# A key or value job that begins in front of the last bank of transposes, in the last block's cross attention of a four-block transformer kernel

## The chip, the cores and the metric

The kernel runs on one core of one Trainium2 chip. A core has a matrix engine (TensorE, "PE" in the profile; its weight loads are "PEld"), three engines for elementwise work (VectorE or "DVE", ScalarE or "ACT", GpSimd or "POOL") and a queue that only issues transfers (SyncE or "SP"). The metric is the device time in microseconds (us) of one execution; less is better. All arithmetic is in 32-bit floats.

## The reference

Four transformer blocks run one after the other on `x` of shape 8 x 112 x 256, with a context of shape 8 x 375 x 192. The first two blocks are self attention, cross attention to the context and a gated feed-forward layer. The third is cross attention alone. The fourth, on which the change works, is

```python
h = _layernorm(x, ln1_w, ln1_b)            # self attention, causal, 16 heads of 16
...
x = x + sa @ proj_w + proj_b
h = _layernorm(x, ln2_w, ln2_b)            # cross attention, 16 heads of 16
q = (h @ q_w + q_b).reshape(B, T, H, HD).transpose(0, 2, 1, 3)
k = (enc @ k_w + k_b).reshape(B, S, H, HD).transpose(0, 2, 1, 3)
v = (enc @ v_w + v_b).reshape(B, S, H, HD).transpose(0, 2, 1, 3)
attn = jnp.einsum('bhtd,bhsd->bhts', q, k) * scale
...
x = x + ca @ out_w + out_b
h = _layernorm(x, ln3_w, ln3_b)
h = jax.nn.gelu(h @ mlp1_w + mlp1_b, approximate=False)
x = x + h @ mlp2_w + mlp2_b
```

with B = 8 batches, T = 112 rows of each, S = 375 context positions, H = 16 heads.

## The kernel before

**Steps.** Attention is cut into 176 steps (0 to 175). In the last block a self-attention step takes 8 heads of one batch, and a cross-attention step 4 heads (four steps to a batch). In Python, each step is a handful of items, made by `add_step` (L913):

- `S`: the score matmuls (L986) into two double-bank PSUM tiles, and, on VectorE, the mask and the row minimum (L934), and half of the step's exponentials on ScalarE (L942). For a cross step these are 4 minima, and 2 of its 4 exponentials, which this text calls the early ones.
- `E`: the other half of the exponentials, the late ones.
- `T`, by bank: four PE transposes of the exponentials (L1013) into one PSUM bank, and the copy of that bank to SBUF. A cross step has three banks (the 375 positions in chunks of 128, 128 and 119): banks 0 and 2 are copied by ScalarE (L1022) and bank 1 by VectorE (L1019). The first bank needs all four exponentials.
- `PV`: the products with the values (L1043), which read the copies.

**Other items.** Projections of the queries (L725), normalizations (`norm`: a product at L669, then statistics on VectorE and GpSimd), their transposes (`hT`, L637), the scaling by the softmax sums (`N`, L1089), and the feed-forward matmuls (`ff`, L1296; made by `last_ff`, L1285) are fillers: the planner puts them between the parts of the steps. ScalarE's exact-GELU passes over the feed-forward result (L1323) are the items `gelu`; the first covers 512 columns in two instructions, the second 256 columns.

**Jobs.** The keys and values of the context (192 deep) are made by jobs in two halves. `begin` issues two matmuls over the first 128 rows (L791 for keys, L866 for values) into two PSUM banks; the second half, called the finish here, issues the two matmuls over the other 64 rows (L800, L875) into the same banks, and then their evacuation. The last block's cross attention has 8 key jobs and 12 value jobs.

**What sets the order.** TensorE's order is the planner's, written out as the program is built (`manual_schedule` for PE, L315). The other engines' queues are ordered by the framework's scheduler, except where the kernel pins an instruction (`keep_in_program_order`, among others for the late exponentials and the GELU passes). [...] The planner's loop (L1468 to L1491) goes through the steps: in iteration i it closes the open jobs (their finish), issues `S` of step i + 2, in every second iteration the `PV` of two steps, then the banks `T` of step i + 1 with fillers between them, `E` of step i + 2, more fillers, and opens jobs at the very end (`open_jobs`, L179). It has a clock of its own with estimated costs: `left` is the filler time due in an iteration, by the fillers' due times, and `ready` (L258) names the filler that can go now, or none. So a shift of one item moves the clock and with it where later fillers go.

**PSUM.** All matmul results other than scores share four banks (`ps_m`, L314), handed out in the order in which they come free. A begun job holds two of them until it is evacuated.

Of the kernel before, what the change touches and what calls it, by code (L numbers as in the profile page):

```python
# [299 lines left out]
def kernel(ctx: ExitStack, tc: tile.TileContext, a: dict, out: bass.AP):  # L300
# [20 lines left out]
    plan = Plan(RINGS, ARENA, lambda k: 512 if k[0] == "v" else S if k[0] == "k" and k[1] in (1, 4, 6, 8) else 4 * T)  # L321
# [845 lines left out]
    def first_of(st, b):  # L1167
        return at[(st, b, 0)]
# [284 lines left out]
    for seg in range(3):  # L1453
        lo, hi = cuts[seg], cuts[seg + 1]


        for s in (lo, lo + 1):
            for k in plan.items[("S", s)].uses + plan.items[("PV", s)].uses:
                mk = plan.maker.get(k)
                if mk is None or plan.items[mk].done:  # L1460
                    continue
                if plan.items[mk].begin is not None:
                    plan.require(mk)
                else:
                    plan.drain(mk)
        if seg == 0:
            plan.require(("hT", 0, 1))
        for i in range(lo - 2, hi):  # L1468
            plan.step = i
            left = plan.pace(i, seg)  # L1470
            if i < lo:

                left = max(left, 6.5)
            plan.close_jobs()
            if lo <= i + 2 < hi:
                plan.main(("S", i + 2))

            if lo <= i < hi and (i - lo) % 2 == 1:
                plan.main(("PV", i - 1))
                plan.main(("PV", i))  # L1480
            if lo <= i + 1 < hi:
                n = steps[i + 1]
                share = left / (n + 2)
                left -= plan.fill(2 * share, 1.5 if i < lo else 0.0)
                for k in range(n):
                    plan.main(("T", i + 1, k))
                    left -= plan.fill(min(left, share))
            if ("E", i + 2) in plan.items and lo <= i + 2 < hi:
                plan.main(("E", i + 2))
            plan.fill(left, 1.5 if i < lo else 0.0)  # L1490
            plan.open_jobs(1 if i + 1 >= first_of(8, 0) else 2, i + 3.5, seg)  # L1491
    plan.step = len(steps)
    while plan.pending:
        plan.drain(plan.pending[0].key)
# [35 lines left out]
```

## Time and profile before

| what | us |
|---|---|
| median of 3 runs (1654.88 to 1657.93) | 1656.19 |
| the profiled execution | 1655.89 |
| its span, first to last instruction | 1654.1 |
| span from 1463 to 1606: last block's attention where jobs are begun, up to the last score matmuls | 143.0, of which PE busy 138.0 |
| span from 1606 to 1614.7: the last steps' transposes and products | 8.7, of which PE busy 6.9 |
| span from 1614.7 to 1651.5: feed-forward tail | 36.8, of which PE busy 36.2 |

The page gives the busy time of each engine; a group line gives the source line, the engine, the operation, the count, the mean, and the idle time before it with what ended it. PE is busy for 99% of the span, DVE 49%, ACT 47%, POOL 43%. Matmul ends are modelled in this profile, so a busy PE does not mean a PE at its fastest; the start times are what is recorded. A timeline row reads: start, length, engine, line, operation, tiles, count, and in brackets the idle time of that engine just before it and what ended it. Rows of several instructions are merged, the start is that of the first. The granted TensorE clock is 1.00 (full) in every slice of the span.

### The profile page before, as it was taken

How to read it: one execution, taken by the hardware profiler on the slowest of the kernel's cores; microseconds unless marked ns; L12 is line 12 of the kernel's file. 1: busy time of each engine (PE TensorE's matmuls, PEld its weight loads, DVE VectorE, ACT ScalarE, POOL GpSimd, SP SyncE). 2: the span in 40 equal slices, each digit the busy share in tenths (PEclk: the TensorE clock that was granted, in tenths of full speed). 3: DMA queues.
4: the chain of work that ended last, by engine and by line, in shares of the span. 5: the costliest groups of instructions: out<-in, count | busy, mean ns of one | idle time of the engine just before them, and what ended most of it. 6: DMA issues, size and time to landing. Idle time of an engine off the chain costs nothing.

```text
span 1654.1 us, 30129 instructions
## 1 busy us (share of the span) xinstructions
PE 1633.6 (99%) x11784; PEld 1142.1 (69%) x11784; DVE 813.6 (49%) x2166; ACT 781.9 (47%) x2448; POOL 718.5 (43%) x687
## 2 busy tenths in 40 slices
PE   9999999999999999999999999999999999999999
PEld 8777666666667878676666665676666666766667
DVE  3554454544522344545454552344455556677752
ACT  3453444444531444434444452144445555687772
POOL 1324555556632223355565580364564448422110
PEclk9999999999999999999999999999999999999999
DMA  6012020000101011000000010100000000000000
GB/s 186 5 54 54 3 87 1 1 26 1 52 29 46 1 30 52 27 1 30 1 2 26 1 46 29 33 23 1 1 2 1 16 1 27 30 2 2 2 2 23
DMA packets 26613, 39.50 MB, mean 24 GB/s; under 512 B 1527, under 2 KB 21623, under 8 KB 26471
## 3 DMA queue, kind: packets, MB, share of 16 engines
q1 hardware_dynamic: 26231, 37.40, 7.3%
q8 instruction: 93, 1.52, 0.4%
q14 instruction: 49, 0.40, 0.1%
q10 hardware_dynamic: 240, 0.17, 0.0%
HBM read 35.88 MB, written 0.92 MB: 22 GB/s over the span
## 4 chain that ended last, share of the span: by engine, by line
PE 90%; ACT 3%; DVE 3%; POOL 2%; issue 1%; ACTq 0%; POOLq 0%; DVEq 0%
PE mm L669 13%; PE mm L703 11%; PE mm L1043 10%; PE s L986 10%; PE mm L1013 9%; PE mm L791 8%; PE mm L825 7%; PE mm L1261 6%; PE mm L800 5%; PE mm L834 4%; PE mm L750 3%; ACT pr L942 2%; PE mm L1296 2%; POOL pr L963 1%; PE mm L637 1%
## 5 line engine op out<-in xcount | busy, mean ns | idle before, releaser
L963 POOL TENSOR_SCALAR pr<-pr,rinv 112x375 f32<-112x375 f32 x384 | 468.7, 1239 | 333.5 <-DVE rinv L960 333.4
L954 ACT ACTIVATE pr<-s,nm 112x375 f32<-112x375 f32 (+1 forms) x640 | 302.0, 489 | 169.4 <-DVE nm L948 167.1
L355 DVE COPY arena<-mm 128x375 f32<-128x375 f32 (+4 forms) x189 | 113.4, 609 | 286.3 <-PE mm L800 137.1
L1013 PEld LDWEIGHTS mm<-ident,pr 112*128 112x128 f32 (+2 forms) x1920 | 209.1, 151 | 50.2 <-issue 19.7
L1013 PE MATMUL mm<-ident,pr 112*128 112x112 f32 (+2 forms) x1920 | 235.4, 264 | 6.8 <-ACT pr L942 3.3
L347 ACT COPY arena<-mm 128x375 f32<-128x375 f32 (+4 forms) x179 | 92.8, 519 | 294.4 <-PE mm L800 139.0
L948 DVE TENSOR_REDUCE nm<-s 112x2 f32<-112x750 f32 (+1 forms) x224 | 206.3, 958 | 51.1 <-PE s L986 47.8
L986 PE MATMUL s<-arena 64*112 64x375 f32 (+3 forms) x1792 | 211.7, 394 | 0.1
L1043 PEld LDWEIGHTS mm<-wT,arena 128*64 128x64 f32 (+5 forms) x3840 | 159.9, 129 | 36.9 <-issue 20.1
L347 ACT COPY wT<-mm 119x448 f32<-119x448 f32 (+2 forms) x235 | 123.8, 535 | 124.5 <-PE mm L1013 124.4
L1043 PE MATMUL mm<-wT,arena 128*64 128x112 f32 (+5 forms) x3840 | 179.5, 261 | 0.0
L986 PEld LDWEIGHTS s<-arena 64*112 64x112 f32 (+1 forms) x1792 | 113.9, 172 | 79.5 <-issue 29.9
L942 ACT ACTIVATE pr<-pr,nm 112x112 f32<-112x112 f32 (+1 forms) x256 | 124.6, 491 | 33.5 <-DVE nm L934 33.5
L969 POOL TENSOR_TENSOR pr<-pr,rinv 112x896 f32<-112x896 f32 x32 | 53.9, 1685 | 197.3 <-DVE rinv L967 179.7
L954 ACT ACTIVATION_READ_ACCUMULATOR pr<-s,nm 112x1 f32 x640 | 133.2, 208 | 0.0
L599 POOL TENSOR_TENSOR rs<-ve,mhalf 128x1 f32<-128x1 f32 x70 | 39.7, 567 | 203.3 <-DVE ve L597 203.3
L960 DVE RECIPROCAL rinv<-sums 112x1 f32<-112x1 f32 x384 | 62.5, 163 | 90.1 <-ACT pr L954 89.6
L825 PE MATMUL mm<-L_xattn_Wv,ctxA 128*128 128x512 f32 (+1 forms) x192 | 92.4, 600 | 2.2 <-ACT wT L347 1.3
L791 PE MATMUL mm<-ctxA,L_xattn_Wk 128*128 128x375 f32 x256 | 91.4, 481 | 0.0
L673 DVE TENSOR_TENSOR x<-mm,x 128x256 f32<-128x256 f32 x70 | 29.6, 423 | 115.9 <-PE mm L669 115.9
L703 PE MATMUL mm<-hT,L_xattn_Wq 128*128 128x224 f32 x384 | 83.0, 360 | 0.0
L353 DVE TENSOR_SCALAR arena<-mm 128x448 f32<-128x448 f32 (+2 forms) x65 | 42.0, 646 | 82.0 <-PE mm L834 47.0
(134 smaller groups left out, 2326.5 us busy)
## 6 DMA issues: line engine op xcount, KB each, us to landing
L_xattn_Wo<-in_L_xattn_Wo_dram SPq DMA_DIRECT2D x3, 1024.0 KB, 15.2
L_xattn_w_ff<-in_L_xattn_w_ff_dram SPq DMA_DIRECT2D x3, 1024.0 KB, 5.2
L_xattn_Wv<-in_L_xattn_Wv_dram SPq DMA_DIRECT2D x4, 512.0 KB, 4.5
L_xattn_Wq<-in_L_xattn_Wq_dram SPq DMA_DIRECT2D x2, 1024.0 KB, 4.7
L_xattn_Wp<-in_L_xattn_Wp_dram SPq DMA_DIRECT2D x2, 1024.0 KB, 5.4
L_xattn_wq<-in_L_xattn_wq_dram SPq DMA_DIRECT2D x2, 1024.0 KB
L_xattn_wo<-in_L_xattn_wo_dram SPq DMA_DIRECT2D x2, 1024.0 KB, 5.3
L_xattn_mlp_w<-in_L_xattn_mlp_w_dram SPq DMA_DIRECT2D x2, 1024.0 KB, 5.3
```

The lines of the kernel that those rows point to most:

```text
L347: nc.scalar.copy(dst, src)
L669: nc.tensor.matmul(ps[:, :D], lhsT=oT[:, c, t * P : (t + 1) * P], rhs=got[wv or w][:, c, :], start=(c == 0), stop=(c == n - 1),)
L703: nc.tensor.matmul(ps[:, i * 2 * T : (i + 1) * 2 * T], lhsT=got[w][:, k, m * P : (m + 1) * P], rhs=hT[:, k, lo:hi], start=(k == 0), stop=( ...
L791: nc.tensor.matmul(ps[:, :S], lhsT=got[wv][:, (2 * u + i) * P : (2 * u + i + 1) * P], rhs=ctxA[:, cols], start=True, stop=False,)
L825: nc.tensor.matmul(ps[: KCH[c][1], :], lhsT=lhs(ctxA, slice(0, KA), c), rhs=got[w][:, hf * 512 : (hf + 1) * 512], start=True, stop=False,)
L942: return nc.scalar.activation(pr, pr, AF.Exp, bias=nm, scale=-1.0, accum_out=bsums[(st, b)][:, h : h + 1])
L948: nc.vector.tensor_reduce(nm[:, :, :ns], sv, AX.X, ALU.max, negate=True)
L954: nc.scalar.activation(pr[:, bk, sl, :], sv[:, bk, sl, :], AF.Exp, bias=nm[:, bk, sl : sl + 1], accum_out=sums[:, bk, sl : sl + 1],)
L963: nc.gpsimd.tensor_scalar_mul(pr[:, bk, sl, :], pr[:, bk, sl, :], rinv[:, bk, sl : sl + 1])
L986: nc.tensor.matmul(tiles[i][:, n % 2, (n // 2) * nk : (n // 2 + 1) * nk], lhsT=qap(h), rhs=kap(h), start=True, stop=True,)
L1013: nc.tensor.transpose(pt[:kl, m * T : (m + 1) * T], cell[h][:, c * P : c * P + kl], ident[:T, :T])
L1043: nc.tensor.matmul(po[p0 : p0 + dp, blk * T : (blk + 1) * T], lhsT=got[vk][:kl, hv * dp : (hv + 1) * dp], rhs=wt, start=(c == 0 and par(h) ...
```

## The change

In the last block (from the iteration whose transposes are those of the first step of its cross attention), in front of a step's last bank of transposes, the planner asks whether any filler is ready. If none is, it opens one job there, sets the remaining filler time of the iteration to nothing, and issues no filler in what is left of the iteration. Where a job was opened in this way, the opening at the end of the iteration opens no second one.

```diff
@@ -1483,12 +1483,19 @@
                 share = left / (n + 2)
                 left -= plan.fill(2 * share, 1.5 if i < lo else 0.0)
                 for k in range(n):
+                    if k == n - 1 and i + 1 >= first_of(8, 0) and plan.ready() is None:
+
+
+                        plan.open_jobs(1, i + 3.5, seg)
+                        left = 0.0
                     plan.main(("T", i + 1, k))
-                    left -= plan.fill(min(left, share))
+                    if not plan.opened:
+                        left -= plan.fill(min(left, share))
             if ("E", i + 2) in plan.items and lo <= i + 2 < hi:
                 plan.main(("E", i + 2))
-            plan.fill(left, 1.5 if i < lo else 0.0)
-            plan.open_jobs(1 if i + 1 >= first_of(8, 0) else 2, i + 3.5, seg)
+            if not plan.opened:
+                plan.fill(left, 1.5 if i < lo else 0.0)
+            plan.open_jobs(1 if plan.opened or i + 1 >= first_of(8, 0) else 2, i + 3.5, seg)
```

As built, nothing differs ahead of step 137. From there on, 13 of the 20 jobs begin in front of the last bank (in the iterations 144, 146, 147, 150, 152, 156, 157, 158, 160, 162, 164, 165 and 166). Fillers shift by an iteration or more: among others the queries `q` of batches 4/5 and 6/7, the norms, and the feed-forward items `ff`, which go to iterations 168 to 171 where they were in 166 to 170. In the last iteration of transposes (174), which has no job to open, the fillers before step 175's last bank are now `hT` (the transposes of rows 512 to 767) and the first `gelu`; before the change both came after it, the `hT` behind the products.

## The prediction

> **What bounds the kernel now.** I read first the busy time of each engine in stretches of the last block (columns: stretch, its length, then PE, PEld, DVE, ACT and POOL busy with instruction counts, granted clock, DMA share, GB/s):
>
> ```profile
> 1463.00:1606.00 143.00, 138.02 (x1467) 90.64 (x1469) 102.40 (x390) 106.78 (x334) 27.65 (x47) 1.00 0.01 2
> 1606.00:1614.71 8.71, 6.89 (x132) 5.17 (x124) 5.36 (x19) 6.43 (x16) 2.92 (x4) 1.00 0.01 2
> 1614.71:1651.50 36.79, 36.24 (x184) 31.86 (x184) 9.37 (x23) 8.19 (x12) 2.51 (x3) 1.00 0.07 22
> ```
>
> PE sets the time in all three. Where jobs move (first row) it is idle for 143.0 - 138.0 = 5.0 us: no order of the same instructions can win more there. The tail (last row) has 0.55 us of PE idle in 36.8, so whatever delays its start delays the end by as much.
>
> Next, who ends PE's waits from 1460 to 1606 (us in total, times, longest):
>
> ```profile
> PE mm L1013 <- ACT pr L942: 2.3, 8, 0.4
> PE mm L791 <- ACT wT L1022: 1.1, 2, 0.6
> PE mm L669 <- ACT wT L1022: 1.0, 2, 0.5
> PE mm L866 <- ACT wT L1022: 0.7, 3, 0.3
> PE mm L791 <- DVE x L673: 0.2, 1, 0.2
> ```
>
> 2.3 of the 5.3 is transposes (L1013) waiting for exponentials, which a moved job does not feed. The rest, 3.0, is jobs and norms that want a PSUM bank and wait for ScalarE's copy of a transposed bank (L1022). These are what the change can reach.
>
> Then single rows: weight loads with the idle time ahead of them.
>
> ```profile
> 1508.86 0.30 PEld L791 LDWEIGHTS mm<-ctxA,ctx_w 128*128 128x128 f32 x2 [1.24 <-ACT wT L1022]
> 1529.45 0.30 PEld L791 LDWEIGHTS mm<-ctxA,ctx_w 128*128 128x128 f32 x2 [1.06 <-ACT wT L1022]
> 1539.77 0.94 PEld L1013 LDWEIGHTS mm<-ident,pr 112*128 112x128 f32 x9 [0.45 <-ACT pr L942]
> ```
>
> In the first two, the second matmul of a key job waits for the PSUM bank that bank 0 of the transposes left; its copy stands on ScalarE behind two early exponentials of the next step (0.60 each). Loads run ahead of matmuls, so PE itself is late by less: measured from start to start, by 0.81 and 0.63.
>
> Last, the end of the attention (step 175), the place that decides my forecast:
>
> ```profile
> 1611.08 1.11 PE L1013 MATMUL mm<-ident,pr 112*128 112x112 f32 x9 [0.28 <-ACT pr L942]
> ...
> 1611.43 0.53 ACT L1022 COPY wT<-mm 128x448 f32<-128x448 f32 x1 [0.41 <-PE mm L1013]
> ...
> 1612.13 1.36 PE L1043 MATMUL mm<-wT,arena 128*32 128x112 f32 x48
> 1612.29 0.53 ACT L1022 COPY wT<-mm 119x448 f32<-119x448 f32 x1 [0.32 <-PE mm L1013]
> 1612.84 1.28 ACT L1323 ACT_TABLE_LOAD   x1
> 1613.42 0.42 PEld L637 LDWEIGHTS mm<-ident,xn 128*128 128x128 f32 x4 [0.17 <-issue]
> ...
> 1614.13 3.71 ACT L1323 ACTIVATE oT<-oT 128x2048 f32<-128x2048 f32 x2
> ...
> 1614.71 7.20 PE L1296 MATMUL mm<-hT,L_xattn_mlp_w 128*128 128x256 f32 x32 [0.64 <-DVE hT L642]
> ```
>
> ScalarE copies banks 0 and 2 of step 175, then loads the GELU table and makes two long GELU passes, under the products and the feed-forward matmuls.
>
> **The change, part by part.** It adds and removes no instruction of PE, DVE, ACT or POOL in sum; no DMA moves, and the queues of SP and POOL keep their order. The built order shows three kinds of shift.
>
> *1. Thirteen jobs begin before the last bank.* The start-to-start spacing in the timeline gives 0.38 for a bank of transposes, 1.26 for a key job's begin, 0.86 for a value job's. Before, PE does banks 1 and 2 and the job's first matmul (0.38 + 0.38 + 0.63 = 1.39) before it wants bank 0's place; after, in most cases, bank 1 and the whole begin (0.38 + 1.26 = 1.64) before the last bank of transposes wants it. So a waiting key job gains 0.25, a value job 0.05 (1.24 against 1.19). Site by site: iterations 144 and 158 gain 0.25 and 0.3, 156 0.1; 146 loses 0.1; the rest waited for nothing. The price: bank 2's copy on ScalarE comes 0.86 to 1.26 later, and the late exponentials of the next step are queued behind it; the next bank 0 waits for these. In ten of the thirteen iterations a pair of `PV` (1.29) stands between, and the late exponentials ended 1.3 to 3.7 ahead of their transposes: hidden. Iteration 147 is a self step whose last bank VectorE copies; 165 is hidden; 157 loses 0.1. Were the cover gone, each would cost up to 0.9. **Sum: gain 0.5.**
> Three key evacuations also go from ScalarE (0.55) to VectorE (0.57), which is idle for 40 of the 143 us: nothing.
>
> *2. Fillers shift.* (a) The queries of batches 6/7 stood between the transposes of step 160 and `S` of 162; their two evacuations on ScalarE held up the late exponentials of 161, and PE lost 0.41 + 0.50 at the transposes (third row above) and 0.15 at the job. Now they follow `S` 162: **gain 1.1**. (b) Steps 151 and 153 lose the filler ahead of their transposes (a norm, 0.97; queries of 4/5, 1.62). From the end of step 150's or 152's bank 2 to the last late exponential it takes 0.2 + 0.53 + 2 x 0.60, and PE has only one `S` (0.83) to put there: new waits of 0.85 and 1.05. At the bank 0 copies behind them 0.3 and 0.5 replace 0.41 and 0.44. The queries, now ahead of step 155's bank 0, remove 0.17 + 0.81 there. 1.83 - 2.70: **loss 0.9**. (c) The norm ahead of job 164 goes behind the products, so that job waits 0.85 and the transposes 0.53 where they waited 0.48; 0.45 is new at 166/167, which lose their feed-forward fillers; these fill 171/172 instead and remove 0.50 and 0.65 around step 173. 1.63 - 1.83: **loss 0.2**.
>
> Parts 1 and 2 gain 0.5 + 1.1 - 0.9 - 0.2 = 0.5 us. Bounds: 5.0 gained (all idle of the first row), and 4 lost (new waits of the size of (b) in every fourth step).
>
> *3. The last iteration.* The norm of tile 5 is now 1.2 us earlier on the planner's clock, so `hT` and the first `gelu` (which asks for 4 us after the last `S`) become ready one bank early and go in front of step 175's bank 2. In the built ScalarE queue, the copy of that bank now stands behind the table load and the two passes. Step 175's last four products (8 of the 48 PE instructions of L1043) need it, and all feed-forward matmuls are queued behind them. From the rows: bank 0's copy ends at 1611.43 + 0.53 = 1611.96; table 1.28: 1613.24; passes 3.71: 1616.95; bank 2's copy 0.53: 1617.48; four products, 0.18, and the change to the next matmul, 0.24: L1296 starts at 1617.9 instead of 1614.71. **Loss 3.2.** The 0.64 wait on hT that goes away is in this difference. PE would have run out of work near 1613.6 (bank 0 ends 1611.2, then 0.38 + 0.5 + 0.4 for banks and `hT`, 1.1 for 40 products), so it stands still for 3.9 us.
>
> Two rules of the Trainium skill bear on this stall, both against the change. The row has the table load at 1.28, starting 0.02 after the copy's end; "ScalarE: Activation LUTs" (What ACT_TABLE_LOAD costs) adds a drain, 2.66 for a switch. By the rule the stall is 1.4 longer and the loss 4.6. I take the row: it is this switch. Second, the clock. No PE pause before the end is over 1.3 us, but behind the last matmul (1650.9) there is one:
>
> ```profile
> 1651.00:1654.10 3.10, 0.00 (x0) 0.00 (x0) 0.42 (x1) 0.00 (x0) 0.00 (x0) 1.00 0.13 42
> 1654.00:1656.00 2.00, 0.00 (x0) 0.00 (x0) 0.00 (x0) 0.00 (x0) 0.00 (x0) 0.70 0.00 0
> ```
>
> 0.70 is 0.8 us at full and 1.2 at half clock: it fell at 1654.8, 3.8 us after the last matmul. "TensorE: Matmul & The Clock Gate" (Part 1) says the same of a free-running idle window of about 3.4 us, and that about 3.4 us of work at half clock restore it. With the row's 3.8, a 3.9 us stall just reaches it; if it does, an estimate from the page is 3.4 / 2 = 1.7 us more. I take nothing and keep it as a rival.
>
> **Sum.** Against the profiled execution: 1655.89 - 0.5 + 3.2 = 1658.6. The median of the runs is 0.3 above that execution, so 1656.19 + 2.7 = 1658.9, said as 1659. About 0.2%, 3.3 us, is what a measurement here tells from no change: the forecast lies just inside it.
>
> **Rivals.**
> - *Not slower:* the bank waits go away at their full size. For it: the five wait rows add to 5.3, and 3.0 of it is at banks. Against it: the last bank then waits for the same copy, and (b) and (c). All idle gone gives -5.0 + 3.2: 1654.4. It decides from a gain of 3.2 on; faster by 0.2% takes more than the 5.0 there are, or a tail that hides its stall.
> - *The clock drops in the stall:* 1659 + 1.7 = 1660.7. For it: 3.9 against 3.8. Against it: the window's place is chance, and the stall may come out shorter.
> - *ScalarE becomes the bound of the steps:* the late copies of bank 2 are not hidden. At 0.4 a site, half of 0.9, for 13 sites: +5, 1664. Against it: ACT is busy 107 of 143, and the slack above. It decides where the slack is under the delay.
> - *Nothing changes:* excluded, since the built order differs.
>
> **How the numbers follow.** Forecast 0.62 (own range 1657.4 to 1660.6; 0.25 of it above 1659.5), not slower 0.13 (0.06 for faster by 0.2%), clock 0.18, ScalarE 0.07. Slower: 0.25 + 0.18 + 0.07 = 0.50; faster 0.06; same 0.44. The range 1655.5 to 1662.5 leaves out most of the ScalarE case and the best of the not-slower one.
>
> **What would show it.** In the profile after: an L1022 copy of 119x448 behind the L1323 passes; a PE wait of 3 to 4 us at L1043 on it, the longest of all; from the first L1296 of 256 columns behind it to the end as before (36.8); PE idle up to the last score matmuls near 4.5 instead of 5.0, with no wait at 1539 and new ones at steps 151 and 153; the granted clock below 1.00 behind the stall or not. Wrong would be a copy that ScalarE makes ahead of the table load, or an attention stretch more than 2 us shorter or longer.

## The result and the profile after the change

| | median us | executions |
|---|---|---|
| kernel before | 1655.57 (1654.88 to 1657.93) | 6 |
| kernel after | 1663.18 (1660.88 to 1663.90) | 6 |

The kernel after takes 1.0042 times as long, 95% interval 1.0032 to 1.0052: slower by 0.42%. The forecast was 1659.0 with a range of 1655.5 to 1662.5: right in direction, too small, and the time is outside the range.

One execution of each kernel is compared first: 1655.89 (span 1654.1) before, 1663.63 (span 1661.8) after. The first view is the busy time in stretches after the change; columns as in the prediction, the clock being the third number from the right.

```profile
1463.00:1606.00 143.00, 137.20 (x1456) 90.53 (x1452) 103.97 (x392) 102.87 (x321) 27.50 (x47) 1.00 0.01 2
1614.71:1651.50 36.79, 33.06 (x193) 28.54 (x192) 9.93 (x24) 7.79 (x7) 2.73 (x4) 0.95 0.05 18
...
1620.00:1625.00 5.00, 4.53 (x20) 3.57 (x21) 1.24 (x3) 0.42 (x2) 0.00 (x0) 0.66 0.00 0
1625.00:1630.00 5.00, 5.00 (x25) 4.41 (x24) 2.72 (x6) 1.06 (x1) 0.00 (x0) 1.00 0.01 3
```

In the first row PE is idle for 5.8 of 143 us where it was 5.0 and I had said 4.5; the tail holds 3.7 us of idle time; and behind it the clock is below full. A second such place lies ahead of everything that the change touches:

```profile
1365.00:1370.00 5.00, 4.95 (x62) 3.02 (x58) 4.55 (x12) 3.12 (x10) 4.94 (x5) 1.00 0.01 3
1370.00:1375.00 5.00, 3.48 (x16) 2.72 (x15) 3.14 (x8) 2.86 (x9) 5.00 (x5) 0.74 0.00 0
1375.00:1380.00 5.00, 5.00 (x47) 3.01 (x48) 2.46 (x5) 1.54 (x5) 2.23 (x3) 0.92 0.00 0
```

The clock records of the trace give both their edges: half clock from 1372.42 to 1375.84 and from 1621.60 to 1625.01, 3.41 us each, 73 x 3.413 us apart. The kernel before has none before its last matmul in its profiled execution. (The profile shows the time ahead of its first clock record, 6.15 us before and 7.09 after, as full clock; the last section comes back to it.)

The timeline of the tail (start, length, engine, line, idle before it):

```profile
1614.45 0.53 ACT L1022 COPY wT<-mm 128x448 f32<-128x448 f32 x1 [0.41 <-PE mm L1013]
...
1615.00 1.28 ACT L1323 ACT_TABLE_LOAD   x1
1615.07 0.57 PE L1013 MATMUL mm<-ident,pr 112*119 112x112 f32 x4
...
1616.29 3.71 ACT L1323 ACTIVATE oT<-oT 128x2048 f32<-128x2048 f32 x2
1619.91 0.51 ACT L1022 COPY wT<-mm 119x448 f32<-119x448 f32 x1
...
1620.47 0.40 PE L1043 MATMUL mm<-wT,arena 119*32 119x112 f32 x8 [3.73 <-ACT wT L1022]
...
1620.80 2.61 PE L1296 MATMUL mm<-hT,L_xattn_mlp_w 128*128 128x256 f32 x7
```

This is the chain of the prediction, link by link: bank 0's copy, the table load, the two GELU passes, and only then bank 2's copy, for which PE stands still 3.73 us. Bank 2 was transposed from 1615.07 on, within 0.6 us; its copy starts at 1619.91, since ScalarE worked its queue in order.

So the 7.7 us between the two spans divide as follows (starts of PE's matmuls; steps by their first score matmul or transpose):

| stretch | before | after | difference | forecast |
|---|---|---|---|---|
| start to `S` of step 146 | 1460.15 | 1462.20 | +2.05 | 0 |
| `S` 146 to the first transpose of step 175 | 149.24 | 150.22 | +0.98 | -0.5 |
| from there to the feed-forward (L1296) | 5.31 | 8.38 | +3.07 | +3.2 |
| from there to the last matmul | 35.87 | 37.52 | +1.65 | 0 |

Only the third row is as forecast. Within the second, the waits of PE from 1460 to 1608 (us in total, times, longest) stand against the five rows of before:

```profile
PE mm L1013 <- ACT pr L942: 2.4, 8, 0.4
PE mm L1013 <- ACT wT L1022: 1.7, 4, 0.6
PE mm L866 <- ACT wT L1022: 0.7, 2, 0.4
PE mm L791 <- ACT wT L1022: 0.3, 1, 0.3
PE mm L1013 <- ACT arena L343: 0.2, 1, 0.2
```

The key jobs (L791) do wait less, 0.3 where it was 1.1. The same wait for the same copy now stands at the transposes (L1013 <- ACT wT L1022, 1.7), which had none before.

### The profile page after: what moved, and what is told of

Same layout as the page of the kernel before. It is cut to its first block, busy times and chain, and to the rows that moved or that the text cites. A ratio compares the mean times of both kernels' runs of the same rounds, so it can differ in the third digit from the quotient of the medians.

```text
span 1661.8 us, 30115 instructions
## 1 busy us (share of the span) xinstructions
PE 1638.1 (99%) x11784; PEld 1146.3 (69%) x11784; DVE 815.4 (49%) x2171; ACT 779.4 (47%) x2443; POOL 716.9 (43%) x687
## 3 DMA queue, kind: packets, MB, share of 16 engines
q8 instruction: 93, 1.52, 0.4%
## 4 chain that ended last, share of the span: by engine, by line
PE 89%; ACT 4%; DVE 4%; POOL 2%; issue 1%; ACTq 0%; POOLq 0%; DVEq 0%
PE mm L669 12%; PE mm L703 11%; PE mm L1043 10%; PE s L986 10%; PE mm L1013 9%; PE mm L791 8%; PE mm L825 7%; PE mm L1261 6%; PE mm L800 5%; PE mm L834 4%; PE mm L750 3%; ACT pr L942 2%; PE mm L1296 2%; POOL pr L963 1%; DVE pr L934 1%
## 5 line engine op out<-in xcount | busy, mean ns | idle before, releaser
L1013 PEld LDWEIGHTS mm<-ident,pr 112*128 112x128 f32 (+2 forms) x1920 | 211.2, 151 | 56.2 <-issue 18.9
L1013 PE MATMUL mm<-ident,pr 112*128 112x112 f32 (+2 forms) x1920 | 239.4, 264 | 8.9 <-ACT pr L942 3.4
L986 PE MATMUL s<-arena 64*112 64x375 f32 (+3 forms) x1792 | 211.7, 394 | 0.1
L986 PEld LDWEIGHTS s<-arena 64*112 64x112 f32 (+1 forms) x1792 | 113.9, 172 | 79.1 <-issue 29.3
L791 PE MATMUL mm<-ctxA,L_xattn_Wk 128*128 128x375 f32 x256 | 92.2, 485 | 0.0
```

The source lines that it names most:

```text
L791: nc.tensor.matmul(ps[:, :S], lhsT=got[wv][:, (2 * u + i) * P : (2 * u + i + 1) * P], rhs=ctxA[:, cols], start=True, stop=False,)
L986: nc.tensor.matmul(tiles[i][:, n % 2, (n // 2) * nk : (n // 2 + 1) * nk], lhsT=qap(h), rhs=kap(h), start=True, stop=True,)
L1013: nc.tensor.transpose(pt[:kl, m * T : (m + 1) * T], cell[h][:, c * P : c * P + kl], ident[:T, :T])
```

## The experiments

In each of these kernels the planner's order is written out as a list from step 137 on and played, so that single items can be moved. In the diffs, `b` is the begin of a job, `kj` and `vj` are key and value jobs, `q` the queries, `N` the scaling, `R` the reciprocal of the softmax sums. A mean clock of .999 over an execution is one window of 3.41 us at half clock, .998 or .997 two or three. Times at 1.000 and at .999 are medians of the executions with that clock; the kernel before, run beside all of them, has 84 executions at 1.000 with 1655.69 (1654.93 to 1656.44) and 20 at .999 with 1658.17. All these ran on several chips; a kernel is set against the runs of before on its own chip where the difference is under 1 us. Times at 1.000 still scatter by 1.5 us, but from `S` 146 to the last matmul the order of before takes 190.41 to 190.42 us in all three profiled executions of it (before, before once more, pause filled). So over this stretch single traces can be compared where no half clock falls into it.

### The kernel before, once more

No edit but the written-out order.

> The order of the kernel before, with nothing changed. The profiled execution after the change has two stretches of 3.41 us at half clock; the earlier one, near 1372 us, lies ahead of every changed instruction. Theory A (it depends on where the clock's windows happen to fall): some executions of the kernel before have it too; these show a mean clock of .999 and 1657 to 1658, the others 1.000 and 1655 to 1656. Theory B (it comes with the change): no execution here is below 1.000, and all lie within 1654.9 to 1656.5.

Measured: 8 of 13 executions at 1.000 (1655.58), 5 at .999 (1658.07). Executions with a half-clock window come without the change too: theory A. They take 2.5 us longer and are about one in five of the kernel before (20 of 104). None of these was profiled; the place near 1372 was seen in three other profiles (after, `tail_alone`, `q_shift_ht`), whose order up to there is that of before.

### The tail alone

```diff
-T 175 1; T 175 2; gelu 9 0; PV 174; PV 175; hT 9 2
+T 175 1; hT 9 2; gelu 9 0; T 175 2; PV 174; PV 175
```

> The kernel before with one change: hT and the first gelu go in front of step 175's last bank of transposes; no job and no filler moves. Theory (the loss is this stall and the half clock behind it): a stall of 3.7 to 3.9 us at the last products, 3.1 us later feed-forward, 1.6 us for half clock: 4.7 over the kernel before, 1660.3, and 1662.3 in executions that also have the half clock near 1372; the mean clock is .999 or .998, never 1.000. Rival (the moved jobs and fillers carry the loss): 1657 or less.

Measured: 3 executions at .999 with 1660.26, 2 at .997 with 1664.0, none at 1.000. The timeline and the stretches of its profile:

```profile
1619.79 0.60 PE L1043 MATMUL mm<-wT,arena 119*32 119x112 f32 x8 [3.73 <-ACT wT L1022]
```

```profile
1615.00:1620.00 5.00, 1.27 (x48) 1.02 (x46) 0.67 (x2) 4.72 (x4) 0.00 (x0) 0.89 0.00 0
1620.00:1625.00 5.00, 5.00 (x19) 3.79 (x12) 1.24 (x3) 0.00 (x0) 0.00 (x0) 0.50 0.00 0
```

With not one job moved, the same 3.73 us stall and half clock behind it, here for two windows. 1660.26 - 1655.69 = 4.6 us of the loss belong to the last iteration alone.

### The first GELU behind the last bank

```diff
 kernel after, iteration 174
-T 175 1; hT 9 2; gelu 9 0; T 175 2; PV 174
+T 175 1; hT 9 2; T 175 2; gelu 9 0; PV 174
```

> The kernel after with one change: the first gelu goes behind step 175's last bank of transposes, so that ScalarE copies that bank ahead of the table load. All moved jobs and fillers stay as in the kernel after. Theory: stall and half clock of the tail are gone, 4.7 less than after: 1656.4 (1658.4 in executions with the half clock near 1372), about 0.9 over the kernel before, since the attention stretch lost 0.9. My own forecast of that stretch (gain 0.5): 1655.1. Rival (the moved jobs carry the loss): 1661 or more.

Measured: 10 of 13 at 1.000 (1656.23), 3 at .999 (1658.24). Moving one item back takes away the whole loss but 0.5 us. The timeline: bank 2's copy is ahead of the table load, and the feed-forward follows without a stall.

```profile
1613.45 0.53 ACT L1022 COPY wT<-mm 119x448 f32<-119x448 f32 x1 [0.76 <-PE mm L1013]
1614.00 1.28 ACT L1323 ACT_TABLE_LOAD   x1
1614.58 6.77 PEld L1296 LDWEIGHTS mm<-hT,L_xattn_mlp_w 128*128 128x128 f32 x32 [0.17 <-issue]
```

The rival (the moved jobs carry the loss) is out. But the attention has not gained: from `S` 146 to step 175's transposes it takes 150.22 us again, 0.98 over the kernel before, and 0.86 of it comes back only from there to L1296, where hT's wait is gone.

### PE kept busy in the stall

```diff
 kernel after, products of step 175 (emit_pv)
                 for c in range(nch):
+                    if s == 175 and c == 2:
+                        warm(15)
                     for h in order[n0 : n0 + nr]:
```

(A call `warm(n)` issues n matmuls of 128x128 on the identity; each shows as two PE instructions.)

> The kernel after with 15 extra 128x128 matmuls on the identity (their result is not used) between the second and the third chunk of step 175's products, where TensorE stands still for 3.7 us. The stall itself stays: the feed-forward's first matmul still waits for ScalarE's late copy. Theory (TensorE's idle time in the stall brings the half clock): no half clock behind it, the feed-forward stretch from its first L1296 to the end 36.8 as in the kernel before and not 38.4; 1.6 less than after, 1659.6 or 1661.6, mean clock one stretch higher than after's. Rival (the clock drops for another reason): stretch 38.4, time as after's, 1663.

Measured: 8 of 9 at 1.000 (1659.51), one at .999. The timeline and the stretch behind the stall:

```profile
1614.36 3.62 PE L381 MATMUL mm<-ident 128*128 128x128 f32 x30
1617.59 0.51 ACT L1022 COPY wT<-mm 119x448 f32<-119x448 f32 x1
...
1618.16 0.40 PE L1045 MATMUL mm<-wT,arena 119*32 119x112 f32 x8 [0.19 <-ACT wT L1022]
```

```profile
1618.80:1655.00 36.20, 35.90 (x184) 31.64 (x182) 8.83 (x23) 5.05 (x10) 2.52 (x3) 1.00 0.07 23
```

The wait for the copy is as long, only filled: the feed-forward starts 3.9 us later than with the GELU behind. Yet the clock stays full. So it is PE's idleness in the stall, and not the delay, that brings the half clock. One window of it costs 1660.88 - 1659.51 = 1.4 us by the one execution that has no other; by the traces, from `S` 146 to the last matmul, 1.7 (196.12 in the kernel after against 194.43 here). This separates the two costs of the tail: 1659.51 - 1656.23 = 3.3 us (3.9 in the profiled pair) for the stall, 1.4 to 1.7 for one window of half clock.

### The kernel after, once more

No edit.

> The kernel after, unchanged. Theory (the stall always brings one stretch of half clock, and the rest is chance): every execution is below 1.000; some at .999 with 1660.5 to 1661.2, the others at .998 or .997, with either the half clock near 1372 too (2.4 longer) or a second window of half clock behind the stall (1.5 to 2 longer). Rival (the change itself brings the half clock near 1372): all at .998 or below, none at .999.

Measured: 4 executions, all at .998: 1662.24, 1662.30, 1662.89, 1663.96. "None at .999" is what the rival said, but the profiled one shows why it is not the rival: full clock at 1372, and two windows at the stall.

```profile
1613.00:1616.70 3.70, 1.55 (x45) 1.20 (x43) 1.16 (x3) 3.69 (x3) 0.00 (x0) 1.00 0.00 0
1616.75:1620.15 3.40, 1.87 (x11) 1.37 (x12) 0.28 (x1) 1.48 (x2) 0.00 (x0) 0.50 0.00 0
1620.20:1623.55 3.35, 3.35 (x9) 2.67 (x8) 0.97 (x2) 0.00 (x0) 0.00 (x0) 0.50 0.00 0
1623.60:1627.00 3.40, 3.40 (x17) 2.98 (x16) 1.81 (x4) 1.06 (x1) 0.00 (x0) 1.00 0.02 5
```

The rows are cut near the edges of its clock windows (the first begins 0.34 us ahead of its window, which is 1613.34 to 1616.75). Of the first, PE is busy for 1.55 of 3.70 and half clock follows; the second has the rest of the stall, busy 1.87 of 3.40, and half clock follows again; the third is busy throughout, and the clock is full. The 3.73 us are shared between two windows, and by how they are cut half clock follows one or both. From `S` 146 to the last matmul this execution takes 196.98 us, so its two windows cost 2.5 against the 194.43 of the filled stall. Over the ten executions of the kernel after one is at .999 (1660.88), five lie between 1662.2 and 1662.9, four between 1663.6 and 1664.0; of these two groups one execution each was profiled (two windows at the stall; one there and one near 1372). That the others of each group are alike is likely, not shown; but nine of the ten, at .998, have two windows by their mean clock.

### The pause near 1370 filled

```diff
 kernel before, transposes (emit_t)
                     pt[:kl, m * T : (m + 1) * T], cell[h][:, c * P : c * P + kl], ident[:T, :T]
                 )
+                if s == 129 and i == 0 and m in (1, 2):
+                    warm(2 if m == 1 else 3)
```

> The kernel before with 5 extra 128x128 matmuls on the identity (result not used) in step 129, two ahead of its third transpose and three ahead of its fourth, where TensorE waits 0.6 and 0.9 us for GpSimd near 1370 us. Theory (these pauses, in one clock window, bring the half clock at 1372): no execution with a mean clock below 1.000; all between 1655.0 and 1656.4, where 10 of 42 executions of the same order were at .999 and 2.4 longer. Rival (it has another cause): about one execution in four at .999 as before.

Measured: 11 of 13 at 1.000 (1655.91), 2 at .999 (1658.21). The pauses are filled (0.15 and 0.21 are left of 0.6 and 0.9), at no cost to the timeline. The kernel before once more, and then this one:

```profile
1370.35 0.32 PE L1013 MATMUL mm<-ident,pr 112*128 112x112 f32 x1 [0.61 <-POOL pr L963]
1371.56 1.12 PE L1013 MATMUL mm<-ident,pr 112*128 112x112 f32 x9 [0.90 <-POOL pr L963]
```

```profile
1369.91 0.62 PE L381 MATMUL mm<-ident 128*128 128x128 f32 x4
1370.69 0.32 PE L1013 MATMUL mm<-ident,pr 112*128 112x112 f32 x1 [0.15 <-POOL pr L963]
1370.84 0.85 PE L381 MATMUL mm<-ident 128*128 128x128 f32 x6
1371.90 1.12 PE L1013 MATMUL mm<-ident,pr 112*128 112x112 f32 x9 [0.21 <-POOL pr L963]
```

But executions at .999 still come. As put, the theory falls: either they have another place too, or the pauses are not the cause. Neither of these two was profiled, so it stays open.

### The thirteen early begins alone

```diff
 kernel before, in each of the 13 iterations
-T n 2; E n+1; b kj 8 5 0; kj 8 5 0
+b kj 8 5 0; T n 2; E n+1; kj 8 5 0
```

(`kj 8 5 0` stands for each iteration's own job, n for its step; a self step's last bank is `T n 1`.)

> The kernel before with one change: the same 13 jobs begin in front of the last bank of transposes; every filler, hT and the gelu stay where they were before. My forecast for this part: a gain of 0.5, so 1655.2 in executions without a half clock, against 1655.7 of the kernel before (each execution with the half clock near 1372 is 2.4 longer). Rival (bank 2's later copy on ScalarE holds up the late exponentials): a loss of 0.5 or more, 1656.2 and above.

Measured: 11 of 13 at 1.000, 1656.35 against 1655.80 of before on the same chip; in the trace `S` 146 to the last matmul is 190.66 against 190.41. So not a gain of 0.5 but a loss: 0.25 by the trace, 0.55 by the medians. Its timeline shows why at the key job of iteration 158, to which I had given 0.3:

```profile
1524.70 0.53 ACT L1022 COPY wT<-mm 119x448 f32<-119x448 f32 x1 [1.24 <-PE mm L1013]
1525.17 0.90 PE L986 MATMUL s<-arena 32*112 32x375 f32 x8
...
1526.52 0.25 DVE L1082 RECIPROCAL rsum<-bsums 112x16 f32<-112x16 f32 x1 [0.50 <-POOL xn L610]
1526.69 0.48 DVE L934 CUSTOM_DVE_ANT_0 pr<-s,cm 112x375 f32<-112x375 f32 x1
...
1528.48 0.51 ACT L1022 COPY wT<-mm 128x448 f32<-128x448 f32 x1
...
1529.04 0.67 PE L1013 MATMUL mm<-ident,pr 112*119 112x112 f32 x4 [0.59 <-ACT wT L1022]
```

The kernel before at this place:

```profile
1526.11 0.90 PE L986 MATMUL s<-arena 32*112 32x375 f32 x8
...
1527.04 0.55 DVE L934 CUSTOM_DVE_ANT_0 pr<-s,cm 112x375 f32<-112x375 f32 x1
```

The early begin of the job before (iteration 157) put step 158's bank 2, and with it its copy (1524.70), behind a value job. The late exponentials of step 159 follow that copy on ScalarE and end at about 1526.4. I had put a loss of 0.1 for this iteration. But VectorE's reciprocal of their sums (L1082) needs them too, and behind it in VectorE's queue stand the minima of the next step (L934), which start 1.52 us after the score matmuls where before it was 0.93. So the next early exponentials are late, and bank 0's copy (1528.48), which is the one the last bank waits for. (The row names GpSimd for the reciprocal's wait; what it reads, the sums, comes from ScalarE.)

### Twelve of them

As above, but `vj 8 4 2` begins behind step 158's last bank again.

> The 13 early begins alone, but one of them (the value job of iteration 157, near 1524) begins at the end of its iteration again. With all 13, step 158's bank 2 copy came 0.9 us later, the late exponentials behind it and VectorE's reciprocal of their sums as well, with the next step's minima queued behind; the bank after the key job at 1529 then waited 0.75 instead of 0.63. Theory: the reciprocal comes in time again, that wait is about 0.25 to 0.4 (0.63 less the forecast's 0.25), and from the score matmuls ahead of it to the first L800 behind it are 3.9 to 4.05 us instead of 4.47 with 13 jobs (4.17 before the change). Rival (the wait is fixed by something else): 0.7 or more, 4.4.

Measured in the timeline (one execution, 1655.70):

```profile
1526.05 0.90 PE L986 MATMUL s<-arena 32*112 32x375 f32 x8
1526.53 0.25 DVE L1082 RECIPROCAL rsum<-bsums 112x16 f32<-112x16 f32 x1
...
1526.98 0.55 DVE L934 CUSTOM_DVE_ANT_0 pr<-s,cm 112x375 f32<-112x375 f32 x1
...
1529.39 0.67 PE L1013 MATMUL mm<-ident,pr 112*119 112x112 f32 x4 [0.25 <-ACT wT L1022]
...
1529.99 0.90 PE L800 MATMUL mm<-ctxB,ctx_w 64*128 64x375 f32 x4
```

The reciprocal no longer waits, the minima start 0.93 after the score matmuls, PE's wait is 0.25 in place of 0.59, and from L986 to L800 it takes 3.94 us: 4.47 with all thirteen, 4.17 before. At this site the gain of a key job's early begin is real (0.23, where I had put 0.25 for such a job and 0.3 for this one), and the begin of the iteration before takes it away.

The whole stretch says more. From `S` 146 to the last matmul it takes 190.14 us: 0.53 less than with thirteen (190.66) and 0.28 less than before (190.41). So the one begin of iteration 157 costs 0.53, and the other twelve gain 0.28 together.

### The shifted fillers without the early begins

```diff
 kernel after, gelu behind step 175's last bank, in each of the 13 iterations
-b kj 8 5 0; T n 2; E n+1; kj 8 5 0
+T n 2; E n+1; b kj 8 5 0; kj 8 5 0
```

> The kernel after with the first gelu behind step 175's last bank, and with the 13 jobs begun at the end of their iterations again, as before; fillers and hT stay as in the kernel after. Together with the 13 jobs it was 1656.2 without a half clock. My forecast for the fillers: 0 for the attention. If the jobs gain their 0.5 and the fillers lose what is missing: 1656.7. If the jobs lose and the fillers do not: 1655.7 or less.

Measured: 12 of 13 at 1.000, 1655.81, the same as before (1655.80 on this chip). In the trace, 150.16 us from `S` 146 to step 175's transposes, 0.92 over the kernel before, and 190.44 to the last matmul, 0.03 over it. So both expectations were too simple: the fillers lose 0.9 in the attention, where I said 0, and hT ahead of the last bank wins it back in the tail. (With the thirteen begins on top, as in `gelu_behind`, the attention takes 0.06 more: the parts do not simply add.)

### hT alone in front of the last bank

```diff
 kernel before, iteration 174
-T 175 1; T 175 2; gelu 9 0; PV 174; PV 175; hT 9 2
+T 175 1; hT 9 2; T 175 2; gelu 9 0; PV 174; PV 175
```

> The kernel before with only hT in front of step 175's last bank (the gelu stays behind it). In the kernels with both fillers and hT moved, the way from step 175's first transposes to the end was 40.3 instead of 41.2. Theory (this is hT's wait of 0.64 that goes, with the bank copies covered): 0.6 to 0.9 less, 1654.8 to 1655.1 in executions at full clock against 1655.75. Rival (those 0.9 are only what the moved fillers had lost ahead of it): 1655.7.

Measured: 10 of 13 at 1.000, 1654.78 against 1655.47 of before on the same chip, 0.7 less; over all executions the ratio is 0.9996 (0.9988 to 1.0004), since the .999 ones widen it. The trace has 189.52 from `S` 146 to the last matmul, 0.9 less. This half of what the change does in the last iteration is a gain.

### And the queries of batches 6/7 behind `S` 162

```diff
 kernel of hT alone
-T 160 2; N 8 3; q 8 3 0; E 161; S 162; norm 9 2; T 161 0
+T 160 2; E 161; S 162; N 8 3; q 8 3 0; norm 9 2; T 161 0
```

> The kernel of ht_alone, with the queries of batches 6/7 and the scaling ahead of them moved behind the score matmuls of step 162. My forecast for these: 1.1 less, 1653.8 at full clock. By the waits of the kernel after (0.26 at the norm and 0.41 behind a query evacuation stand where 0.41 + 0.50 + 0.15 went away): 0.3 to 0.4 less, 1654.5.

Measured: 6 of 13 at 1.000 with 1653.88, 7 at .999 with 1656.55; median of all 1655.87. At full clock that is 0.9 less than hT alone (0.63 in the trace), nearer to the forecast of 1.1 than to the 0.3 that I had read from the kernel after. The two waits that stand in the kernel after (0.26 for the scaling, 0.41 for a bank with a query in it) are not here: there the norm also moved, to between bank 0 and bank 1. That it is the norm was not tried alone. Why 7 of 13 had the half-clock window is not known; the profiled one had it near 1372.

### All three edits together

The order of `q_shift_ht` with the five matmuls of `pause_filled` in step 129.

> The kernel of q_shift_ht with the 5 extra matmuls of pause_filled in step 129 (their result is not used). At full clock as q_shift_ht, 1653.9, that is 1.6 less than the kernel before. Of executions at .999: if the pause near 1370 is what brings them, at most one in 13; if they come from elsewhere, as the 2 of 13 of pause_filled suggest, two to four; if the order of q_shift_ht itself brings them, about seven as there.

Measured: median 1654.21 over 13 executions, ratio 0.9989 (0.9981 to 0.9998); 11 at 1.000 with 1654.17 (before on the same chip 1655.33), 2 at .999. At full clock that is 1.2 less than before (1.5 from `S` 146 to the last matmul, 188.89), where I said 1.6. This is the one version that is faster than both kernels beyond its interval, by 0.1%. With `pause_filled` that makes 4 of 26 at .999, against 20 of 104 of the kernel before: no sign that the filled pause helps. Against the 7 of 13 of `q_shift_ht`, on another chip, 2 of 13 are fewer, but too few executions to say.

## Why the prediction was wrong

**The last iteration was right.** The forecast had the feed-forward 6.47 us after bank 0's copy (1611.43 to 1617.9) and a loss of 3.2; it was 6.35 (1614.45 to 1620.80) and 3.1. `tail_alone` and `gelu_behind` show by putting it in and taking it out, and `ht_alone` by moving hT without it, that it is this one item, the GELU. The table load took 1.28 and started 0.02 behind the copy's end, as the row had it; the 2.66 that "ScalarE: Activation LUTs" (What ACT_TABLE_LOAD costs) of the Trainium skill gives for a switch would have been too long.

**"I take nothing" for the clock was the failed step.** The forecast compared a stall of 3.9 us with the 3.8 us after which the clock fell behind the last matmul, and called the drop a matter of chance. It was none: 15 of 15 executions with the stall (after, after once more, the tail alone) are below 1.000, and `busy_stall` shows the cause. The comparison failed because the 3.8 is where a drop was seen, not what a drop needs.

The records show fixed windows of 3.413 us, and what fits them best is how much of one window is idle. I counted as idle what passes from 0.30 us after a matmul's start to the next start, where the starts are over 0.33 apart. In the profiles of all kernels here, the windows with half clock behind them (up to the last matmul) have 1.57 to 2.79 us of it (from 1.59 on where the window itself is at full clock). No window with 1.54 or less has half clock behind it. Of those above that, only four of 1.65 and 1.66 near 1390 have none, so this count does not part the two cleanly. A stall of 3.7 us puts half of itself, 1.87, into some window however it is cut.

The likeliest value should have had one window, and its price was well sized: 1.7 forecast, 1.4 to 1.7 measured. With one alone the time is within the range (1660.88). What I had not thought of is a second window, at the stall or near 1372: nine of ten executions of the kernel after have two, and take 1662.2 to 1664.0.

**Part 1, "gain 0.5", had the wrong sign.** Alone it loses 0.25 to 0.55. The step that failed is "157 loses 0.1": that begin costs 0.53, and without it the other twelve gain 0.28. I looked for who waits at the transposes for late exponentials, and not at VectorE, where a reciprocal waits for them with the minima behind it. `twelve_jobs` shows that for this site; the other twelve were not taken apart.

**Part 2, 0 in sum, cost 0.9.** (a) is right when it is alone (0.6 to 0.9 of 1.1); in the kernel after 0.26 + 0.41 come back, where the norm moved with it, which I did not cost. (b) is right in its places and nearly in size: steps 151 and 153 wait 0.27 + 0.49 and 0.51 + 0.49 at the transposes where I said 0.85 and 1.05. (c) also: in `fillers_alone`, 0.50 at step 165's transposes and 0.65 at the job behind them for 0.53 and 0.85, and 0.63 near 1570 for 0.45. So 0.7 of the 0.9 are the two waits that came back; the rest is spread too thin to name. With the jobs on top the attention is 0.98 longer, where the sum said 0.5 shorter.

Two readings of the lines were off. Of the 3.0 us put down to ScalarE's bank copies, 0.2 (the last of the five rows) waits for VectorE. And PE does not set the time in the second of the three stretches, where it is busy for 6.89 of 8.71 us: `ht_alone` won its 0.9 there.

**The sum again.** 3.1 for the stall, 1.0 for the attention and 1.65 for the clock make 5.7 of the 7.7 in the profiled pair. The remaining 2.0 are the window near 1372, which this execution has and that of before has not, and a start some 0.4 later (last section); both lie ahead of the first changed instruction. At full clock throughout, as `busy_stall` has it, the kernel would stand at 1659.5 against my 1659.0: the misses in parts 1 and 2 are within the range, and it is the clock that leaves it. That the two are so near is in part luck: the 1656.19 from which I counted had an execution of 1657.93 in its three and lies 0.5 above the 1655.69 at full clock, which hides a third of the 1.5 missed in parts 1 and 2.

Of the rivals, "the clock drops" was the nearest (1660.7), with 0.18 of the chance. "ScalarE becomes the bound of the steps" has its mechanism in `jobs_alone`, through VectorE, at a tenth of its price.

## What to carry to other kernels

When one item slips ahead of a copy on an in-order engine, follow everything that reads the copy and everything queued behind those readers, on every engine and not only on the critical one: here the minima queued behind a reciprocal came 0.6 us later, and with them the next step. A stall of the matrix engine has a second price, the clock behind it; here half clock followed windows of 3.41 us of which 2.2 to 2.8 were idle. Whether two pauses of 0.6 and 0.9 us in one window do the same is open. And before a difference of 2 us in two traces is put down to an edit, look whether it begins ahead of the first changed instruction.

## What the runs showed of the hardware that was not expected

The half clock does not need a whole idle window. "TensorE: Matmul & The Clock Gate" (Part 1) of the Trainium skill speaks of an idle window of about 3.4 us; here, at the stall, windows with 2.16 to 2.79 us of idle time had half clock behind them, and filling the stall removed it. Near 1372, windows with 1.59 to 1.63, less than half, had it too, though there the cause is open. It lasted one or two whole windows of 3.413 us.

Whether the kernel meets it near 1372 us goes with where its windows lie. Counted from the first instruction, the windows begin at some offset within 3.413 us. The three profiled executions that have the half clock there lie at 0.27, 0.69 and 0.97; the other eleven, at 1.11 to 3.25, have none there. That leaves a band of 0.7 to 1.3 us out of 3.41, 21 to 37% if the offset is chance; the kernel before has a half-clock window in 19% of its executions (20 of 104). In those three both pauses near 1370 lie in one window; in the nine others that have the pauses unfilled, an edge parts or cuts them and no window there has over 1.54 us. That four of 26 executions with the pauses filled are at .999 does not fit, unless the clock falls elsewhere in these; the windows near 1390, with up to 1.66, would be a candidate, but none was profiled. So this is a correlation, with its cause open.

The same offset sets the start. The identity matmuls at the head of the program start 0.21 us apart up to the first clock record and 0.11 behind it: the kernel starts at half clock, and full clock comes at 4.52 us (`fillers_alone`) to 7.80 (`tail_alone`). `S` 146 comes at 1459.3 to 1460.2 in the eleven, the later the later full clock came (but for one pair 0.13 apart). The three with the window near 1372 are those where it came last (7.09 to 7.80). So the 2.5 us of such executions are two things: against `ht_alone`, whose order is the same up to there, `q_shift_ht` loses 1.7 in the window itself and 0.4 at the start.
